# Graph attention on one core: edge attributes in another layout, masks for four tiles at once, one-hots on ScalarE, and second operands of VectorE in PSUM

## The chip, the cores and the metric

The kernel runs on one core of one Trainium2 chip. The metric is the time that the device takes for one execution, in microseconds (us). TensorE (PE) multiplies matrices and loads its weights (PEld); VectorE (DVE) and ScalarE (ACT) work element by element; GpSimd (POOL) here does little but issue gathers, that is, DMAs whose source rows are given by an index; SyncE (SP) issues the other DMAs. SBUF and PSUM are the two on-chip memories.

## The reference

A graph has N = 12500 nodes with 128 features and E = 200000 edges, sorted by their target node. Two layers follow each other, each added to its input:

```python
h = jnp.maximum(_layernorm(x, axis=-1), 0.0)
x = x + _L0_gnn_ref(h, edge_index, edge_attr_32, Wq, Wk, Wv, We)     # attention over edges
h = jnp.maximum(_layernorm(x, axis=-1), 0.0)
x = x + _L1_gnn_ref(h, edge_index, ...)                              # three graph convolutions
```

The change concerns the attention alone:

```python
q = (x @ Wq.T).reshape(N, H, C)          # H = 8 heads, C = 16; k and v alike
edge_bias = edge_attr @ We.T             # (E, 32) @ (32, 8)
scores = jnp.einsum('ehc,ehc->eh', q[dst], k[src]) / np.sqrt(C) + edge_bias
seg_max = jax.ops.segment_max(scores, dst, num_segments=N)
ex = jnp.exp(scores - seg_max[dst])
denom = jax.ops.segment_sum(ex, dst, num_segments=N)
out = segment_sum(v[src] * (ex / denom[dst])[:, :, None], dst)
```

## The kernel before

The program has a general path and a path for graphs whose edges are sorted and evenly spread (`fast()`); the second one runs here. Three stages follow each other.

**Start.** The first edge of each node tile is found (`sv`, `begin`, L193 to L203), and q, k and v of all nodes are computed and written to DRAM (`q_d`, `kv_d`).

**Attention** (L893 to L1132). The nodes are cut into 106 tiles of 118 (`TN`). Each tile takes a window of 2048 edges (`WE`) from the first edge of its nodes on, laid out as 128 partitions times 16 edges (`JJ`). A loop over groups of four tiles prepares masks (`cut`, `con`, `thru`, L976 to L996) and, inside it, each tile does the following. The names are those that the profile's rows show.

- SP loads the edge attributes `ebx` (L1003), the numbers of the target nodes in the tile spread over all partitions, `dw_b` (L1005), and the tile's queries `qt` (L1007). The place of the first edge goes through a one-element copy on ACT (`first_edge`, L929) into a register of SP.
- POOL issues 16 gathers of 128 rows of `kv_d`, 1 KB each (L148, called from `gather`); `kv` has three buffers.
- DVE makes the one-hot `oht` (nodes x edges, L1013). Sixteen matmuls spread the queries to the edges (`qe`, L1019), DVE multiplies them with the keys (L1020) and sums over C (L1023).
- TensorE transposes `ebx` (L1029), ACT copies the result (`et`, L1032), and four matmuls with `wbd` give the bias (L1036), which DVE adds to the scores (L1038).
- ACT spreads the mask `cut` over the heads (`cm`, L1043, L1045). DVE finds the segment maximum by scans along the 16 edges of a partition (L1051, L1053). The ends of the partitions go through TensorE (`ends`, L1058 to L1061), are scanned across the partitions (L1067, L1069) with `th`, a copy that ACT makes of the transposed `thru` (L1065), come back (`far`, L1071, L1072), and the first scans are repeated.
- ACT takes the exponential and writes it into column C of `vals` in SBUF (L1081). DVE multiplies the values with it (L1082, both inputs in SBUF).
- DVE makes the other one-hot, `oh` (edges x nodes, `one_hot`, L677), and sixteen matmuls sum up (`acc`, L1089), which ACT copies to `att` (L1090).

**Sorting beside it.** From the 25th tile on a generator `place_edges` (L680 to L888) does work for the third stage: it sorts 2048 keys of each tile, all 106 tiles side by side in 106 partitions, by two bitonic sorts of 66 exchanges each (`swap`, L700 to L702: one minimum and one maximum over 1024 elements, all operands in SBUF), and then places the result by shifts. `go_on(1)` stands at four places of a tile and advances the generator by one `yield`, which is one exchange, or one of the later instructions.

**Convolutions** (L1190 on): three times, gathers of `t_d` (POOL), one-hots on DVE (`oh`, L1249, whose constant operand `nums` lies in PSUM) and matmuls.

A scheduler sets the order of the instructions of each engine at build time; at run time every engine takes its own in that order and waits by semaphores.

Of the kernel before, what the change touches and what calls it, by code (L numbers as in the profile page):

```python
# [17 lines left out]
P = 128  # L18
D = 128
H = 8  # L20
# [28 lines left out]
def tile_gnn(ctx: ExitStack, tc: tile.TileContext, x, src, dst, ea, wqkvT, weT, w1, w2, w3, par, out):  # L49
# [16 lines left out]
    assert E % RR == 0 and E >= WE and NTT < P and (NTT - 1) * TN + P <= NP  # L66
# [38 lines left out]
    begin = const.tile([1, P], I32, name="begin")  # L105
    way = const.tile([1, 1], I32, name="way")
# [44 lines left out]
    with ExitStack() as s:  # L151
# [44 lines left out]
        nc.vector.tensor_tensor(sv[:, 2 * P:2 * P + NTT], sv[:, 1:NTT + 1], sv[:, 0:NTT], op=ALU.subtract)  # L196
# [5 lines left out]
        nc.vector.tensor_scalar(sv[:, :P], sv[:, :P], float(E - WE), None, op0=ALU.min)  # L202
        nc.vector.tensor_copy(begin, sv[:, :P])  # L203
# [454 lines left out]
    def fast():  # L658
# [21 lines left out]
        def place_edges(rt, ps):  # L680
# [10 lines left out]
            def turned(a, n, o, copy):  # L691

                av = a[:, :n * P].rearrange("t (p c) -> t c p", c=n)
                for c, m in groups(n, 4):
                    tp = ps.tile([P, 4, P], FP, name="et_p")
                    for i in range(m):
                        nc.tensor.transpose(tp[:, i, :NTT], av[:, c + i, :], ident[:NTT, :NTT])
                    copy(o[:, :, c:c + m].rearrange("p t c -> p c t"), tp[:, :m, :NTT])

            def swap(lo, hi, lo2, hi2):  # L700
                nc.vector.tensor_tensor(lo2, lo, hi, op=ALU.min)
                nc.vector.tensor_tensor(hi2, lo, hi, op=ALU.max)  # L702

            def sort(turn):
                size = 2
                while size <= WE:
                    a, b = (x.rearrange("t (n z) -> t n z", z=size) for x in (A[turn], A[1 - turn]))
                    h = size // 2
                    swap(a[:, :, :h], a[:, :, h:][:, :, ::-1], b[:, :, :h], b[:, :, h:][:, :, ::-1])
                    yield  # L710
                    turn = 1 - turn
                    d = h // 2
                    while d:
                        a, b = (x.rearrange("t (n w d) -> t n w d", w=2, d=d) for x in (A[turn], A[1 - turn]))
                        swap(a[:, :, 0], a[:, :, 1], b[:, :, 0], b[:, :, 1])
                        yield
# [43 lines left out]
            mb = ps.tile([P, 2, MG], FP, name="nb")  # L760
            nc.tensor.matmul(mb[0:1, 0, 0:1], sm[:, 3:4], ones[:NTT, 0:1], start=True, stop=True)
            yield
            nc.vector.tensor_scalar(slotted, mb[0:1, 0, 0:1], 0.0, None, op0=ALU.is_equal)
# [121 lines left out]
        with ExitStack() as s:  # L885
# [10 lines left out]
            ps1 = s.enter_context(tc.tile_pool(name="ps1", bufs=1, space=PSUM))  # L896

# [14 lines left out]
            nc.vector.tensor_scalar(shift[:, 1], iota_f, pid[:, 2:3], None, op0=ALU.is_equal)  # L912
            NV = 2
# [12 lines left out]
            def first_edge(bg, t):  # L926


                nc.scalar.copy(bg, begin[:, t:t + 1])  # L929
                return nc.values_load(bg, engines=[mybir.EngineType.SP], min_val=0, max_val=E - WE)  # L930
# [34 lines left out]
            for t0 in range(0, NTT, NG):  # L965
                n = min(NG, NTT - t0)
                if t0 % MG == 0:
# [5 lines left out]
                    if loaded >= NTT and not steps:  # L973
                        steps = place_edges(rt, ps1)
# [10 lines left out]
                    nb = ps1.tile([P, 2, MG], FP, name="nb")  # L985
# [9 lines left out]
                    for m in (con, thru):  # L995
                        nc.vector.tensor_scalar(m[:, :, :mn], m[:, :, :mn], BIG, -BIG, op0=ALU.mult, op1=ALU.add)  # L996
                att = ep.tile([TN, NG, H * (C + 1) + 1], FP, name="att")
                for t in range(t0, t0 + n):
                    i, m = t - t0, t - m0
                    ebx = ld.tile([P, JJ * ED + 1], FP, name="ebx")  # L1000
                    eb = ebx[:, :JJ * ED].rearrange("p (j w) -> p j w", j=JJ)
                    v = first_edge(ebx.bitcast(I32)[0:1, JJ * ED:], t)
                    nc.sync.dma_start(eb, ea[bass.ds(v, WE), :].rearrange("(p j) w -> p j w", j=JJ))  # L1003
# [9 lines left out]
                    nc.vector.tensor_scalar(oht, dw_b, iota_q, None, op0=ALU.is_equal)  # L1013
# [11 lines left out]
                    go_on(1)  # L1025

                    et_p = ps1.tile([P, 4, P], FP, name="et_p")
                    for k in range(4):
                        nc.tensor.transpose(et_p[:, k, :], eb[:, 4 * k:4 * k + 4, :].rearrange("p j w -> p (j w)"),  # L1029
                                            ident)  # L1030
                    et = wk.tile([P, 4, P], FP, name="et")
                    nc.scalar.copy(et, et_p)  # L1032
                    sm = ps1.tile([P, JJ + 2, H], FP, name="sm")
                    bias, far = sm[:, :JJ], sm[:, JJ:]
                    for k in range(4):
                        nc.tensor.matmul(bias[:, 4 * k:4 * k + 4, :].rearrange("p j h -> p (j h)"), et[:, k, :], wbd,  # L1036
                                         start=True, stop=True)
# [3 lines left out]
                    cm = wk.tile([P, H * (JJ + 1) + 1], FP, name="cm")  # L1041
                    W = H * (JJ + 1)
                    nc.scalar.copy(cm[:, :W].rearrange("p (h j) -> p h j", h=H),  # L1043
                                   cut[:, m, :].unsqueeze(1).to_broadcast([P, H, JJ + 1]))
                    nc.scalar.copy(cm[:, W:], cut[:, m, JJ:])  # L1045
# [11 lines left out]
                    ends = ps1.tile([H, 4, P], FP, name="ends")  # L1057
                    nc.tensor.matmul(ends[:, 0, :], mg[:, :, JJ - 1], ident, start=True, stop=True)  # L1058
                    nc.tensor.matmul(ends[:, 1, :], mx[:, :, 0], ident, start=True, stop=True)
                    for k in range(2):  # L1060
                        nc.tensor.matmul(ends[:, 2 + k, :], thru[:, k, m:m + 1].to_broadcast([P, H]), ident,  # L1061
# [388 lines left out]
```

## Time and profile before

| | us |
|---|---|
| time, median of 3 runs (7284.83 to 7306.85) | 7293.77 |
| the profiled execution's own time | 6154.56 |
| its span, first to last instruction | 6152.8 |
| first gather of `kv` begins | 148.2 |
| first and last exchange of the sorts begin | 743.9, 1728.1 |
| last gather of `kv` begins | 2930.9 |
| last copy of `att` (end of the last tile) begins | 2958.1 |

The profiled execution was 1139.2 us shorter than the median of the timed ones; the records do not say why. All durations below are the profiled execution's.

Busy time by stretch, from the profile's windows (first column: stretch in us; then its length, and the busy time of PE, DVE, ACT and POOL; the TensorE clock as a share of full speed; the mean share of the DMA engines that was busy):

| stretch | tiles begun in it | length | PE | DVE | ACT | POOL | clock | DMA |
|---|---|---|---|---|---|---|---|---|
| 148 to 721 | 24 | 573 | 399.95 | 357.29 | 84.00 | 446.40 | 0.72 | 0.58 |
| 721 to 2544 (sorting) | 66 | 1823 | 1165.11 | 1385.66 | 225.80 | 1499.36 | 0.69 | 0.44 |
| 2544 to 2931 | 16 | 387 | 276.01 | 225.00 | 50.85 | 305.37 | 0.69 | 0.48 |
| 2958 to 6153 (convolutions) | | 3195 | 2454.93 | 1297.12 | 598.64 | 1827.63 | 0.88 | 0.82 |

A row of the groups names the source line, the engine, the operation, the tile written and those read, the shapes and the count; after the bar come the busy time in us and the mean duration of one in ns; after the second bar the idle time of the engine just before these instructions, and what ended most of it. "issue" means that the profile shows nothing that the engine waited for. In a timeline each row has its start in us, its duration in us, and then the same names.

### The profile page before, as it was taken

How to read it: one execution, taken by the hardware profiler on the slowest of the kernel's cores; microseconds unless marked ns; L12 is line 12 of the kernel's file. 1: busy time of each engine (PE TensorE's matmuls, PEld its weight loads, DVE VectorE, ACT ScalarE, POOL GpSimd, SP SyncE). 2: the span in 40 equal slices, each digit the busy share in tenths (PEclk: the TensorE clock that was granted, in tenths of full speed). 3: DMA queues.
4: the chain of work that ended last, by engine and by line, in shares of the span. 5: the costliest groups of instructions: out<-in, count | busy, mean ns of one | idle time of the engine just before them, and what ended most of it. 6: DMA issues, size and time to landing. Idle time of an engine off the chain costs nothing. (4 is left out here: it accounts for less than half of the span.)

```text
span 6152.8 us, 80384 instructions
## 1 busy us (share of the span) xinstructions
PE 4406.0 (72%) x28564; PEld 4115.5 (67%) x28564; DVE 3396.2 (55%) x5972; ACT 1011.7 (16%) x2374; POOL 4084.2 (66%) x3617
## 2 busy tenths in 40 slices
PE   6676666666666665767487787877787787778777
PEld 2666655555566665666377777777777776777777
DVE  7566688887876677655243343353343344434344
ACT  3111111110111111111112122111121211112120
POOL 0777788888888888777266566636666664666663
PEclk9677766666676776767788888898888888888888
DMA  6555544433444444454588888878888887888888
GB/s 188 152 143 138 137 112 106 113 103 109 105 128 120 122 112 112 131 132 114 150 214 216 218 216 218 213 209 217 219 216 221 213 211 204 219 219 219 221 215 209
DMA packets 607714, 1051.07 MB, mean 171 GB/s; under 512 B 191227, under 2 KB 418491, under 8 KB 607201
## 3 DMA queue, kind: packets, MB, share of 16 engines
q1 hardware_dynamic: 464311, 695.85, 41.5%
q0 software_dynamic: 142608, 348.39, 23.9%
q8 instruction: 232, 3.80, 0.3%
q14 instruction: 175, 1.43, 0.1%
q10 hardware_dynamic: 388, 1.60, 0.1%
HBM read 773.19 MB, written 272.26 MB: 170 GB/s over the span
## 5 line engine op out<-in xcount | busy, mean ns | idle before, releaser
L148 POOL DMA_INDIRECT rows<-t_d,srcO x1908 | 1827.6, 958 | 1329.2 <-issue 560.2
L148 POOL DMA_INDIRECT kv<-kv_d,srcA x1696 | 2252.3, 1328 | 536.7 <-issue 484.3
L1249 DVE TENSOR_TENSOR oh<-nums,dlS 128x1888 f32<-128x1888 f32 x318 | 674.3, 2121 | 1527.2 <-PE zp L1255 1517.9
L1253 PE MATMUL zp<-oh,mr 128*128 128x118 f32 x6360 | 966.6, 319 | 567.5 <-DMA mr<-m 440.4
L1253 PEld LDWEIGHTS zp<-oh,mr 128*128 128x128 f32 x6360 | 925.5, 233 | 586.4 <-DMA mr<-m 348.7
L1019 PE MATMUL qe<-qt,oht 128*128 128x128 f32 x3392 | 841.4, 415 | 247.3 <-DVE kv L1020 110.7
L1224 PE MATMUL gp<-hs,go 128*117 128x128 f32 x7056 | 891.8, 281 | 125.8 <-DVE go L1221 69.8
L1019 PEld LDWEIGHTS qe<-qt,oht 128*128 128x128 f32 x3392 | 767.1, 310 | 289.7 <-issue 166.8
L1224 PEld LDWEIGHTS gp<-hs,go 128*117 128x117 f32 x7056 | 831.9, 184 | 165.1 <-issue 117.1
L1226 ACT COPY stage<-gp 117x512 f32<-117x512 f32 x1008 | 521.8, 532 | 1375.0 <-PE gp L1224 936.8
L1020 DVE TENSOR_TENSOR kv<-qe,kv 128x512 f32<-128x512 f32 x424 | 289.4, 685 | 678.8 <-DMA kv<-kv_d,srcA 536.8
L1089 PE MATMUL acc<-vals,oh 128*118 128x137 f32 x3392 | 539.8, 329 | 150.5 <-DVE vals L1082 150.0
L1089 PEld LDWEIGHTS acc<-vals,oh 128*118 128x118 f32 x3392 | 522.1, 225 | 171.6 <-DVE vals L1082 171.3
L1221 DVE TENSOR_SCALAR go<-gi,iota_q 128x468 f32<-128x468 uint8 x1008 | 427.8, 456 | 224.5 <-DMA gi<-gi_d 111.8
L1255 PE MATMUL zp<-oh,rows 128*128 128x118 f32 x3816 | 513.2, 288 | 0.2 <-DMA rows<-t_d,srcO 0.2
L1255 PEld LDWEIGHTS zp<-oh,rows 128*128 128x128 f32 x3816 | 492.2, 206 | 0.4 <-DMA rows<-t_d,srcO 0.4
L1058 PE MATMUL ends<-ident,mg 128*8 128x128 f32 x212 | 53.0, 343 | 344.4 <-DVE mg L1053 305.6
L1082 DVE TENSOR_TENSOR vals<-kv,vals 128x2048 f32<-128x2048 f32 x106 | 242.3, 2286 | 27.2 <-ACT vals L1081 26.8
L1058 PEld LDWEIGHTS ends<-ident,mg 128*8 128x8 f32 x212 | 11.7, 96 | 366.1 <-DVE mg L1053 298.8
L1023 DVE TENSOR_REDUCE sc<-kv 128x128 f32<-128x2048 f32 x106 | 240.8, 2272 | 0.0
L677 DVE TENSOR_TENSOR oh<-iota_f,dlA 128x1888 f32<-128x1888 f32 x106 | 224.0, 2113 | 5.0 <-PE acc L1089 5.0
L1036 PE MATMUL sm<-wbd,et 128*128 128x32 f32 x848 | 167.8, 351 | 45.0 <-DVE mg L1075 37.7
(242 smaller groups left out, 3648.1 us busy)
## 6 DMA issues: line engine op xcount, KB each, us to landing
m<-stage SPq DMA_DIRECT2D x252, 784.0 KB
mr<-m SPq DMA_DIRECT2D x318, 560.0 KB
dw_b<-dlb_d SPq DMA_DIRECT2D x106, 512.0 KB
gi<-gi_d SPq DMA_DIRECT2D x252, 204.8 KB
rows<-t_d,srcO POOLq DMA_INDIRECT x1908
kv<-kv_d,srcA POOLq DMA_INDIRECT x1696
ebx<-in_edge_attr_dram SPq DMA_DIRECT2D x106, 256.0 KB
mr<-m SPq DMA_DIRECT2D x318, 75.0 KB
```

The source lines that it names most:

```text
L148: nc.gpsimd.indirect_dma_start(out=o, out_offset=None, in_=table[:, :], in_offset=bass.IndirectOffsetOnAxis(ap=idx, axis=0))
L1019: nc.tensor.matmul(qe[:, k, :], ohv[:, :, j + k], qt, start=True, stop=True)
L1020: nc.vector.tensor_tensor(qk[:, j:j + 4, :], qe, qk[:, j:j + 4, :], op=ALU.mult)
L1023: nc.vector.tensor_reduce(sc.rearrange("p h j -> p j h"), qk.rearrange("p j (h c) -> p j h c", h=H), AX.X, ALU.add)
L1082: nc.vector.tensor_tensor(vh[:, :, :, :C], kv[:, :, D:].rearrange("p j (h c) -> p j h c", h=H), vh[:, :, :, C:].to_broadcast([P, JJ, H, C] ...
L1089: nc.tensor.matmul(acc, oh[:, j, :], va[:, j, :], start=(j == 0), stop=(j == JJ - 1))
L1221: nc.vector.tensor_scalar(go[:, :n], gv[:, a:a + n], iota_q, None, op0=ALU.is_equal)
L1224: nc.tensor.matmul(gp[:, i, :], go[:, i].rearrange("p t k -> p (t k)"), hs[:, g * SG + a + i, :], start=True, stop=True)
L1226: nc.scalar.copy(stage[:, a:a + n, :], gp[:, :n, :])
L1249: nc.vector.tensor_tensor(oh, nums.unsqueeze(1).to_broadcast(sh), dlS[:, t, :].unsqueeze(2).to_broadcast(sh), op=ALU.is_equal)
L1253: nc.tensor.matmul(zp[:, i, :], mr[:q, j, :], oh[:q, j, :], start=False, stop=False)
L1255: nc.tensor.matmul(zp[:, i, :], rows[:, j, :], oh[:, RC + j, :], start=False, stop=(j == JO - 1))
```

## The change

- **Edge attributes.** A second input holds the attributes transposed: row 32·i + w, column e holds attribute w of edge 4·e + i. A tile loads 128 rows of 512 columns (`eaT`), 256 KB as before, and multiplies them with `wbd` directly; the four transposes and the copy `et` go. The first edge of a tile is rounded down to a multiple of 4 for this (`begin4`).
- **Masks.** `cm` and `th` are made for a group of four tiles ahead (`cms`, two `th2`), not once a tile.
- **One-hots on ACT.** `oht` and `oh` are made by ACT as relu(1 - |x - y|): an Abs with a bias per partition and a Relu in place; `oh` needs 16 of the Abs, one for each edge of a partition.
- **Exponentials in PSUM.** ACT writes the exponentials to PSUM (`ex`), DVE multiplies the values from there, and ACT copies `ex` into `vals`.
- **Sort halves in PSUM.** Each exchange is cut into two halves. For each, ACT copies the upper operand to PSUM (`hc`, one buffer), a `yield` follows, and DVE takes minimum and maximum of an SBUF and a PSUM operand. `go_on` advances six steps a tile in place of four.
- **PSUM.** `ends` and the tile `sm` (bias, `far`, `ex`) have two buffers each, `acc` one.

```diff
             def swap(lo, hi, lo2, hi2):
-                nc.vector.tensor_tensor(lo2, lo, hi, op=ALU.min)
-                nc.vector.tensor_tensor(hi2, lo, hi, op=ALU.max)
+                n, d = lo.shape[1:]
+                for k in range(2):
+                    cut = (slice(None), slice(k * n // 2, (k + 1) * n // 2)) if n > 1 else (
+                        slice(None), slice(None), slice(k * d // 2, (k + 1) * d // 2))
+                    hc = ps.tile([P, WE // 4], FP, name="hc")[:NTT].rearrange(
+                        "t (n d) -> t n d", n=max(1, n // 2))
+                    nc.scalar.copy(hc, hi[cut])
+                    yield
+                    nc.vector.tensor_tensor(lo2[cut], lo[cut], hc, op=ALU.min)
+                    nc.vector.tensor_tensor(hi2[cut], lo[cut], hc, op=ALU.max)
...
+            def where_zero(x):
+                nc.scalar.activation(x, x, AF.Relu, bias=ones[:, 0:1], scale=-1.0)
...
+                    cms = mk.tile([P, MG, W + 1], FP, name="cms")
+                    nc.scalar.copy(cms[:, :mn, :W].rearrange("p m (h j) -> p m h j", h=H),
+                                   cut[:, :mn].unsqueeze(2).to_broadcast([P, mn, H, JJ + 1]))
+                    nc.scalar.copy(cms[:, :mn, W:], cut[:, :mn, JJ:])
+                    ths = {}
+                    for a, b in groups(mn, 2):
+                        th2 = mk.tile([H, 2, 2, P], FP, name="th2")
+                        ends = ps2.tile([P, 4, P], FP, name="ends")[:H]
+                        for i in range(2 * b):
+                            nc.tensor.matmul(ends[:, i, :], thru[:, i % 2, a + i // 2:a + i // 2 + 1]
+                                             .to_broadcast([P, H]), ident, start=True, stop=True)
+                        nc.scalar.copy(th2[:, :b].rearrange("h m k p -> h (m k) p"), ends[:, :2 * b])
...
-                    nc.sync.dma_start(eb, ea[bass.ds(v, WE), :].rearrange("(p j) w -> p j w", j=JJ))
+                    nc.sync.dma_start(eb, eaT[:, bass.ds(v, WE // 4)])
...
-                    nc.vector.tensor_scalar(oht, dw_b, iota_q, None, op0=ALU.is_equal)
+                    nc.scalar.activation(oht, dw_b, AF.Abs, bias=niota[:, 0:1])
+                    where_zero(oht)
...
-                    go_on(1)
-                    et_p = ps1.tile([P, 4, P], FP, name="et_p")
+                    go_on(2)
+                    sm = ps2.tile(shared, FP, name="sm")
+                    bias, far, ex = sm[:, :JJ], sm[:, JJ:JJ + 2], sm[:, JJ + 2:]
                     for k in range(4):
-                        nc.tensor.transpose(et_p[:, k, :], eb[:, 4 * k:4 * k + 4, :].rearrange("p j w -> p (j w)"),
-                                            ident)
-                    et = wk.tile([P, 4, P], FP, name="et")
-                    nc.scalar.copy(et, et_p)
...
-                        nc.tensor.matmul(bias[:, 4 * k:4 * k + 4, :].rearrange("p j h -> p (j h)"), et[:, k, :], wbd,
-                                         start=True, stop=True)
+                        nc.tensor.matmul(bias[:, 4 * k:4 * k + 4, :].rearrange("p j h -> p (j h)"),
+                                         eb.rearrange("a (p k) -> a k p", k=4)[:, k, :], wbd, start=True, stop=True)
...
-                    nc.scalar.activation(vh[:, :, :, C], mx.rearrange("p h j -> p j h"), AF.Exp)
+                    nc.scalar.activation(ex, mx.rearrange("p h j -> p j h"), AF.Exp)
                     nc.vector.tensor_tensor(vh[:, :, :, :C], kv[:, :, D:].rearrange("p j (h c) -> p j h c", h=H),
-                                            vh[:, :, :, C:].to_broadcast([P, JJ, H, C]), op=ALU.mult)
+                                            ex.unsqueeze(3).to_broadcast([P, JJ, H, C]), op=ALU.mult)
+                    nc.scalar.copy(vh[:, :, :, C], ex)
                     go_on(1)
                     oh = wk.tile([P, JJ, TN], FP, name="oh")
-                    one_hot(oh, dlA[:, t, :])
-                    acc = ps2.tile([TN, H * (C + 1) + 1], FP, name="acc")
+                    for j in range(JJ):
+                        nc.scalar.activation(oh[:, j, :], iota_f[:, :TN], AF.Abs, bias=dlA[:, t, j:j + 1], scale=-1.0)
+                    where_zero(oh)
+                    acc = ps1.tile([TN, H * (C + 1) + 1], FP, name="acc")
```

## The prediction

> **What bounds the kernel now.** The chain of waits of the page tells nothing here: it ends after five short steps. I read first the costliest groups, then the timeline, then the windows.
>
> ```profile
> L148 POOL DMA_INDIRECT rows<-t_d,srcO x1908 | 1827.6, 958 | 1329.2 <-issue 560.2
> L148 POOL DMA_INDIRECT kv<-kv_d,srcA x1696 | 2252.3, 1328 | 536.7 <-issue 484.3
> ```
>
> Second row: POOL's gathers of the attention. Busy 2252.3 plus idle 536.7 is 2789 us, and by their first and last start they last from 148.2 to 2930.9, 2783 us. So POOL does nothing but issue gathers, one after another with 0.305 us between, and nearly never waits: **attention is as long as 1696 gathers take to issue.** Nothing of the third stage starts before it ends, so a microsecond saved there is one saved in all. The first row is the same instruction in the convolutions: 958 ns in place of 1328. Why, the timeline shows, first in attention, then in a convolution:
>
> ```profile
> 342.31 0.95 POOL L148 DMA_INDIRECT kv<-kv_d,srcA  x1 [0.30 <-issue]
> 343.56 0.95 POOL L148 DMA_INDIRECT kv<-kv_d,srcA  x1 [0.30 <-issue]
> 343.89 2.29 DVE L1082 TENSOR_TENSOR vals<-kv,vals 128x2048 f32<-128x2048 f32 x1 [3.11 <-ACT vals L1081]
> ...
> 344.82 2.19 POOL L148 DMA_INDIRECT kv<-kv_d,srcA  x1 [0.30 <-issue]
> ...
> 347.31 0.94 POOL L148 DMA_INDIRECT kv<-kv_d,srcA  x1 [0.30 <-issue]
> ```
>
> The convolution:
>
> ```profile
> 4004.05 2.12 DVE L1249 TENSOR_TENSOR oh<-nums,dlS 128x1888 f32<-128x1888 f32 x1 [1.97 <-PE zp L1255]
> ...
> 4004.50 0.94 POOL L148 DMA_INDIRECT rows<-t_d,srcO  x1 [0.30 <-issue]
> 4005.74 0.94 POOL L148 DMA_INDIRECT rows<-t_d,srcO  x1 [0.30 <-issue]
> ```
>
> The gather at 344.82, issued while DVE multiplies two SBUF operands, ends 0.83 us after DVE does; its neighbours take 0.95. In the convolution, under a DVE operation as long but with one operand in PSUM (`nums`), gathers keep 0.94. I set all 1696 gathers of the timeline against DVE's intervals: the 648 that meet L1082, L677, L1013, L701 or L702 take 1849 ns in the mean, the 1048 others 1006. Above the usual 947 that is 584 us for the first and 62 us for the second. These five lines are what the change takes out of VectorE's SBUF operands.
>
> By the windows a tile takes 573/24 = 23.9 us at first, 1823/66 = 27.6 beside the sorting, 387/16 = 24.2 at the end.
>
> **POOL after the change.** L1082 and the exchanges get a PSUM operand, L677 and L1013 leave DVE. Nearest row for the first two: L1020, kv<-qe,kv, has one PSUM and one SBUF input; fitted over all gathers, a gather loses about a tenth of its overlap with it, against nine tenths for L1082. So all gathers should come to the mean of the unhindered 1048: 16 x (1.006 + 0.305) = 21.0 us a tile. The ends: 16 x (0.947 + 0.305) = 20.0 if nothing hinders, 27.6 in the sorting if PSUM operands hindered as well. I take 21.0; scans (L1051, L1053), L1078 and the placing after the sorts keep two SBUF inputs and are in it. All 1696: 2223 us against 2783, **560 us less, if no other engine is slower than 21 us a tile.**
>
> Here the Trainium skill speaks against the change. "SBUF — State Buffer", Who interferes with whom, says that VectorE with two SBUF inputs holds up only GpSimd instructions that read SBUF, and infers that descriptor generation, being a write, is held up by two-port modes alone. By that rule only L1013 (tensor_scalar on bf16, 106 x 1.28 = 136 us at most) would matter, and the change would bring about 100 us. The rows above contradict it: L1082 is a tensor_tensor, and the gather under it took 2.19 us. I go by the trace.
>
> **ACT.** Rows to price from, of ACT's groups within the attention:
>
> ```profile
> L1032 ACT COPY et<-et_p 128x512 f32<-128x512 f32 x106 | 62.1, 586 | 551.2 <-PE sm L1036 472.2 <-PE et_p L1029 78.9
> L1081 ACT ACTIVATE vals<-mg 128x128 f32<-128x128 f32 x104 | 44.5, 428 | 27.2 <-DVE mg L1078 25.9
> L1126 ACT ACTIVATE hg<-xg,rs 118x128 f32<-118x128 f32 x100 | 41.2, 482 | 132.0 <-DVE rs L1122 132.0
> L1065 ACT COPY th<-ends 8x256 f32<-8x256 f32 x105 | 38.0, 362 | 394.8 <-PE ends L1061 394.8
> ```
>
> From L1065 to L1032, 256 elements more cost 224 ns, 0.875 ns each. So 2048 elements are 586 + 1536 x 0.875 = 1.93 us, 1888 are 1.79. `oht`: two passes, 3.86. `oh`: sixteen Abs over 118 elements; L1126 (118 x 128, two pointers) starts every 0.386 us in a row, so at most 6.2 us; "ScalarE: Activation LUTs", What ACT_TABLE_LOAD costs, takes 93 ns off for one pointer less, an estimate of 4.7; I take 5.0, and the Relu 1.79. The copy of `ex` is priced like L1081, 0.43; `Exp` stays. Gone are `et` 0.59, `th` 0.36, `cm` 0.49, against two copies like L1032 and one `cms` per four tiles, about 0.5. ACT now has 360.66/106 = 3.4 us a tile; after: 3.4 - 1.44 + 3.86 + 5.0 + 1.79 + 0.43 + 0.5 = 13.5. In the sorting six `hc` copies of 512 elements come on top; nearest row 0.586 (end above: 1.2, at the 1.9 ns that an element of the strided L1081 costs beyond its start): 3.5, so **17.0 us**. That is below 21, but no longer idle.
>
> The same page's rules for authors say to use VectorE, not ScalarE, for relu and the like. Rows: DVE makes both one-hots in 1.28 + 2.11 = 3.4 us, ACT needs 10.65. By the rule the edit loses 7 us of engine time a tile, 770 us in all; but ACT was busy 13% of the attention and DVE's 3.4 us sit on POOL, which sets the pace. By the trace the edit gains, as long as ACT stays below POOL.
>
> **DVE.** Now 14.9 us a tile (357.29/24) outside the sorting, 21.0 in it. The one-hots go: 11.5. In the sorting six half exchanges a tile, each two operations like L1020 at 0.685: 8.2, so **19.7 us** (somewhat less, since successive operations overlap by some 0.08). All 132 exchanges cost 4 x 0.685 - 2.42 = 0.32 more each, 43 us over the whole, beside POOL. Six steps a tile with twice the yields per exchange: the sorts take 264/6 = 44 tiles (before, 984 us), the placing fewer than before, and the generator ends near the same tile; nothing spills over the end.
>
> **PE.** The transposes go (L1029: 424, 105.8 us); the same matmuls on `thru` are only moved to the group. PE's 1841.07 us become some 1735, 16.4 a tile. The weights `eb` are read with a step of four elements; `oht` is read with sixteen, and its loads (310 ns against 225 for `acc`) hide beside matmuls. DMAs: as many, as large; their share of 0.44 to 0.58 rises by the shorter tile to 0.6 to 0.67, and the convolutions reach 0.82 on the same engines. SP's queue keeps its order; its register loads wait for the one-element ACT copies, now behind operations of up to 1.93 us, with two tiles of lead. Five small DVE instructions for `begin4` cost about 1 us ahead of the first gather. One `acc` buffer: the next tile's sum waits for the ACT copy of the last, a tile earlier.
>
> **The new wait.** An `hc` copy needs DVE to have finished with the one buffer; in ACT's queue one-hots and `Exp` stand behind it, and TensorE waits for those. DVE's minimum needs the copy; queued behind it are scans, score products and the `vals` product that frees `kv`. Six round trips a tile: two half operations 1.37, copy 0.59. Other work between two trips: DVE (19.7 - 8.2)/6 = 1.9 us, ACT (17.0 - 3.5)/6 = 2.3. If they mesh perfectly, a trip costs about 3.3 to 3.5 us and a tile 20 to 21; if half of the copies stand behind an ACT operation of 1.9 us with little else to do on DVE, about 3 us a tile are added. I take **23.3 in the sorts, 22 in the placing, 21 elsewhere**: 44 x 23.3 + 22 x 22 + 40 x 21 = 2349 us against 2783, 434 less. In the profiled execution 6154.56 becomes about 5720.
>
> The runs' median is 1139.2 us above the profiled execution, and no view says why. Carried over unscaled, 434 us give 6860; scaled by 7293.77/6154.56 = 1.185, 514 us give 6780. I take the middle, **6820**.
>
> **Rivals.**
> - *POOL alone sets the pace* (18%): DVE and ACT mesh; 560 to 660 less, 6630 to 6730. For it: in the sorting before DVE was busy 76% and POOL did not wait. Against it: two more engines at 80 to 94%.
> - *The handing over of `hc` sets the pace, yet below the old one* (18%): 25 to 27 us a tile while sorting; 66 x (27.6 - 26) + 40 x 2.9 = 222 less, 7070.
> - *Slower* (13%): the same hand-over, each copy behind a long ACT operation. With 19.7 us of DVE work and six idle times a tile, the sorting tile passes the point where the other tiles' 116 us are eaten at 27.6 + 116/66 = 29.4 us, that is at 1.6 us idle per copy. With 2.5 us (a 1.93 us Relu and the copy) it is 34.7: 66 x 7.1 - 116 = 353 more, 7650. Against it: DVE's scans and products usually stand between.
> - *It does not do what it says*: the skill's rule holds, -100 us at best, or PSUM operands hinder too (3%, counted as no change).
>
> **Chances.** Main case 48%. A change within 0.3% (22 us) is about what a measurement of this kernel can't tell from none. Faster 84%, same 3%, slower 13%. The range 6600 to 7190 leaves out the slower case and the weakest of the partial ones; the main case's own range is 6720 to 6920.
>
> **What would show it.** Gathers of `kv` near 1.0 us in place of 1.33; POOL's idle time before them up, ended by DVE (a `kv` buffer not free) in the sorting if hand-over slips; ACT busy about 2200 us in place of 1011.7; the last gather starting near 2500. Wrong would be: gathers that stay at 1.3 us, ACT rows above 2.5 us for 2048 elements, or DVE idle more than 1.6 us before each minimum.

## The result, and the profile after

The changed kernel takes 7762.7 us (median of 4 runs, 7753.7 to 7795.7) where the kernel before takes 7289.3 (7274.2 to 7306.9) on the same chip: a ratio of **1.068 [1.064, 1.071]**. It is slower; the forecast was 6820 us.

What the change says it does, it did. Of the profile page after, the costliest groups that answer to those shown before (line, engine, operation, tiles, shapes, count; busy us, mean ns; idle us before, and what ended most of it):

```profile
L149 POOL DMA_INDIRECT rows<-t_d,srcO x1908 | 1823.7, 956 | 2328.9 <-PE zp L1184 666.8
L149 POOL DMA_INDIRECT kv<-kv_d,srcA x1696 | 1695.3, 1000 | 1696.5 <-DVE vals L1104 847.0
...
L1114 PE MATMUL acc<-vals,oh 128*118 128x137 f32 x3392 | 616.9, 352 | 507.7 <-ACT vals L1106 263.4
...
L1056 DVE TENSOR_TENSOR kv<-qe,kv 128x512 f32<-128x512 f32 x424 | 285.4, 678 | 565.5 <-remote 357.9
...
L1115 ACT COPY att<-acc 118x137 f32<-118x137 f32 x106 | 29.0, 273 | 921.4 <-remote 452.3
```

Second row: a gather of `kv` takes 1000 ns in place of 1328, so POOL issues all 1696 in 557 us less. But its idle time went from 536.7 to 1696.5 us, and half of that is now ended by the `vals` product, which frees a `kv` buffer: POOL no longer sets the pace. No other engine does so by its work alone: of the 3431 us of attention TensorE is busy 1907, VectorE 1662 and ScalarE 1512. The word "remote" at the last two rows is new: the first profile of the kernel before has no such wait. It is what the profile writes where the awaited signal came, but so late (over 1.5 us after the recorded end of every instruction that sends it) that it names no sender. The first row, the convolutions' gathers, is untouched by the change, yet waits 2328.9 us where the profile before had 1329.2.

ACT's groups have the sizes that the prediction gave them:

```profile
L1110 ACT ACTIVATE oh<-iota_f,dlA 128x118 f32<-128x118 f32 x1696 | 510.3, 382 | 0.0
L1048 ACT ACTIVATE oht<-dw_b,niota 128x2048 f32<-128x2048 bf16 x106 | 211.7, 1998 | 95.7 <-PE qe L1055 58.9 <-remote 33.1 <-issue 2.9
...
L930 ACT ACTIVATE oh<-oh,ones 128x1888 f32<-128x1888 f32 x106 | 197.2, 1860 | 7.2 <-remote 6.1 <-ACT oh L1110 0.6 <-ACT oht L1048 0.4
L712 ACT COPY hc<-A 106x512 f32<-106x512 f32 x264 | 156.6, 593 | 334.7 <-DVE A L715 268.7 <-issue 37.2 <-DVE A L714 21.6
```

Where the time goes is seen in the timeline of the changed kernel (start, duration, engine, line; in brackets the idle time before and what ended it), here ahead of the sorting:

```profile
400.24 2.28 DVE L1104 TENSOR_TENSOR vals<-kv,sm 128x2048 f32<-128x2048 f32 x1
...
400.88 0.95 POOL L149 DMA_INDIRECT kv<-kv_d,srcA  x1 [0.30 <-issue]
...
402.55 0.38 ACT L1106 COPY vals<-sm 128x128 f32<-128x128 f32 x1 [5.30 <-issue]
...
404.13 1.03 PE L1055 MATMUL qe<-qt,oht 128*128 128x128 f32 x4
404.64 0.94 POOL L149 DMA_INDIRECT kv<-kv_d,srcA  x1 [0.30 <-issue]
405.42 0.01 SPq L958 DMA_DIRECT2D srcA<-in_src_dram  x1
405.89 0.95 POOL L149 DMA_INDIRECT kv<-kv_d,srcA  x1 [0.30 <-issue]
406.85 0.70 SPq L959 DMA_DIRECT2D dwx<-dstf_d  x1
...
433.42 0.95 POOL L149 DMA_INDIRECT kv<-kv_d,srcA  x1 [0.30 <-issue]
434.28 0.28 ACT L1115 COPY att<-acc 118x137 f32<-118x137 f32 x1 [31.05 <-remote]
...
434.61 5.54 PE L1114 MATMUL acc<-vals,oh 128*118 128x137 f32 x29 [29.44 <-issue]
...
444.21 0.69 DVE L1056 TENSOR_TENSOR kv<-qe,kv 128x512 f32<-128x512 f32 x1 [33.08 <-PE qe L1055]
```

and in the windows over the gap (busy us and number of instructions of each engine, granted clock, DMA share):

```profile
core 0: us, PE busy (x) PEld busy (x) DVE busy (x) ACT busy (x) POOL busy (x), PEclk, DMA share, GB/s
...
404.00:434.00 30.00, 1.16 (x7) 0.97 (x5) 0.61 (x3) 0.00 (x0) 22.68 (x25) 0.56 0.43 111
```

The last matmul of a sum ends at 404.30, the next tile's sum needs the one `acc` buffer, and ACT's copy out of it comes 30 us later. TensorE's 12 records of that window (weight loads included) all lie before 405.2; after them it records nothing for 29.4 us, VectorE three instructions and ScalarE none, and SP issues one load in 1.4 to 8.4 us, in place of one in about 0.5. Only POOL works on, one gather per 1.25 us. VectorE stands idle for over 10 us in one piece 52 times in the 106 tiles (three times in the first profile before). Attention, from the first gather to the last copy of `att`, takes 3431 us in this execution.

**Two kinds of chip.** Five further series of runs, each on another chip, always had the kernel before beside them. On four chips it took 7286 to 7389 us, on one 6150 (medians; on one chip single runs lie within 1.2% of each other). Each chip had one series, so what is called a kind of chip here could also be a condition of the machine at that hour; no run tells the two apart. The profile that the prediction was read from shows 6154.56, like the odd one; the times it was to forecast are of the other kind. So before anything else the kernel before was profiled again.

### The profile page after: what moved, and what is told of

It is laid out like the page before. It is cut to its first block, busy times and chain, and to the rows that moved or that the text cites. A ratio compares the mean times of both kernels' runs of the same rounds, so it can differ in the third digit from the quotient of the medians.

```text
span 7766.9 us, 81306 instructions
## 1 busy us (share of the span) xinstructions
PE 4783.1 (62%) x28140; PEld 4417.7 (57%) x28140; DVE 3091.8 (40%) x6028; ACT 2165.5 (28%) x4439; POOL 3523.3 (45%) x3617
## 5 line engine op out<-in xcount | busy, mean ns | idle before, releaser
L149 POOL DMA_INDIRECT rows<-t_d,srcO x1908 | 1823.7, 956 | 2328.9 <-PE zp L1184 666.8
L149 POOL DMA_INDIRECT kv<-kv_d,srcA x1696 | 1695.3, 1000 | 1696.5 <-DVE vals L1104 847.0
L1249 PE MATMUL gp<-hs,go 128*117 128x128 f32 x7056 | 1078.6, 312 | 689.0 <-issue 506.3
L1278 PE MATMUL zp<-oh,mr 128*128 128x118 f32 x6360 | 1057.7, 337 | 602.6 <-DMA mr<-m 317.6
L1249 PEld LDWEIGHTS gp<-hs,go 128*117 128x117 f32 x7056 | 979.9, 212 | 772.4 <-issue 617.1
L1278 PEld LDWEIGHTS zp<-oh,mr 128*128 128x128 f32 x6360 | 1014.6, 251 | 623.3 <-issue 356.8
L1110 ACT ACTIVATE oh<-iota_f,dlA 128x118 f32<-128x118 f32 x1696 | 510.3, 382 | 0.0
L1066 PE MATMUL sm<-wbd,ebx 128*128 128x32 f32 x848 | 209.9, 393 | 160.2 <-DMA sw_d<-srcA 62.6
L1066 PEld LDWEIGHTS sm<-wbd,ebx 128*128 128x128 f32 x848 | 208.7, 328 | 162.5 <-issue 125.1
L712 ACT COPY hc<-A 106x512 f32<-106x512 f32 x264 | 156.6, 593 | 334.7 <-DVE A L715 268.7
L1104 DVE TENSOR_TENSOR vals<-kv,sm 128x2048 f32<-128x2048 f32 x106 | 241.5, 2278 | 9.0 <-ACT sm L1103 4.4
```

Source lines behind the costliest of these rows:

```text
L149: nc.gpsimd.indirect_dma_start(out=o, out_offset=None, in_=table[:, :], in_offset=bass.IndirectOffsetOnAxis(ap=idx, axis=0))
L1110: nc.scalar.activation(oh[:, j, :], iota_f[:, :TN], AF.Abs, bias=dlA[:, t, j:j + 1], scale=-1.0)
L1249: nc.tensor.matmul(gp[:, i, :], go[:, i].rearrange("p t k -> p (t k)"), hs[:, g * SG + a + i, :], start=True, stop=True)
L1278: nc.tensor.matmul(zp[:, i, :], mr[:q, j, :], oh[:q, j, :], start=False, stop=False)
```

## Experiments

### First series (kernel before: 7365.6 us)

`again_before` is the kernel before. `onehots_dve` takes both one-hots back to VectorE, `sort_sbuf` the exchanges back to SBUF (with `go_on(1)`), `both_back` does both:

```diff
-                    nc.scalar.activation(oht, dw_b, AF.Abs, bias=niota[:, 0:1])
-                    where_zero(oht)
+                    nc.vector.tensor_scalar(oht, dw_b, iota_q, None, op0=ALU.is_equal)
...
-                    for j in range(JJ):
-                        nc.scalar.activation(oh[:, j, :], iota_f[:, :TN], AF.Abs, bias=dlA[:, t, j:j + 1], scale=-1.0)
-                    where_zero(oh)
+                    one_hot(oh, dlA[:, t, :])
...
-                    yield from swap(a[:, :, :h], a[:, :, h:][:, :, ::-1], b[:, :, :h], b[:, :, h:][:, :, ::-1])
+                    swap(a[:, :, :h], a[:, :, h:][:, :, ::-1], b[:, :, :h], b[:, :, h:][:, :, ::-1])
+                    yield
```

> The kernel before, unchanged, for a profile that belongs to the timed runs. Theory S (the first profile of before, 6153 us, was an execution without TensorE's late progress that the profile of the changed kernel shows): span near 7290 us, convolutions near 4180 us in place of 3195, attention (first gather to last att copy) 2950 to 3150 us. Rival (the convolutions of the changed kernel are slower because of the change): the convolutions stay near 3200 us and the span cannot be explained by them.

> The changed kernel with both one-hots back on VectorE (tensor_scalar and tensor_tensor as before), all else as changed. Theory A (ScalarE's order of work, with 10.6 us of one-hots a tile in front of Exp, vals and att copies, delays TensorE and so the release of kv): attention falls from 3430 us to 2750 or less and the time to 7050 to 7200, below the kernel before. Theory B (the hand-over of hc): no more than 100 us change, 7650 to 7760. Theory S alone (late TensorE, whatever the order): about 7700.

> The changed kernel with the exchanges of the sorts as before (two SBUF operands, one yield each, four steps a tile). Theory B: the tiles beside the sorting fall from 31 us to 25, the time to about 7350. Theory A: the tiles without sorting take 33.6 us in the changed kernel too, so the sorting is not the cause; within 100 us of 7763, and gathers in the sorting become longer.

> The changed kernel with one-hots on VectorE and exchanges as before; what stays of the change is the layout of the attributes, the masks for four tiles and the exponentials in PSUM. Theory A: near the kernel before, 7100 to 7300, since only the product of the values no longer holds up gathers (about 190 us less of hindrance) and no ScalarE queue is added. If it stays above 7500, the cause lies in the remaining parts: the tile sm that is shared by bias, far and ex, or one buffer of acc.

Measured: `again_before` 7374.7 us (1.002 [1.000, 1.004]), `onehots_dve` 7582.4 (1.028 [1.020, 1.036]), `sort_sbuf` 7814.6 (1.059 [1.053, 1.066]), `both_back` 7534.7 (1.022 [1.017, 1.028]).

The kernel before spends 2963 us in attention and 4232 in the convolutions on this chip, against 2810 and 3194 in its first profile, while the mean gather differs little (1298 against 1328 ns, and 955 against 958 in the convolutions). So 1038 us of the 1139 that the prediction could not place lie in the convolutions. They are not only waits: TensorE's granted clock there is 0.79 in place of 0.88, and its busy time 2766 us in place of 2455. And the changed kernel (4182 there) doesn't lengthen them: its loss is all in attention, 3431 against 2963.

The hand-over of `hc`, the prediction's slower rival, is not the cause: without it attention stays at 3420 us, and the 24 tiles ahead of the sorting are as slow as those beside it (33.9 and 32.0 us a tile in the changed kernel). The one-hots are a half: 3184 us of attention without them, still more than before, while the range expected was missed. This run alone does not say that ScalarE's time is the reason, for with VectorE's one-hots back the gathers take 1125 ns in place of 1000, so that their pace changes too. What `both_back` keeps (layout, masks, `ex` in PSUM, one `acc`) costs 2.2% on its own.

### Second series (kernel before: 6150.5 us)

`acc_two` is `both_back` with two `acc` buffers, `ex_back` is `both_back` with the exponentials written into `vals` and not copied, `layout_masks` is both, `before_acc1` is the kernel before with one `acc` buffer:

```diff
-                    acc = ps1.tile([TN, H * (C + 1) + 1], FP, name="acc")
+                    acc = ps2.tile([TN, H * (C + 1) + 1], FP, name="acc")
...
-                    nc.scalar.activation(ex, mx.rearrange("p h j -> p j h"), AF.Exp)
+                    nc.scalar.activation(vh[:, :, :, C], mx.rearrange("p h j -> p j h"), AF.Exp)
...
-                                            ex.unsqueeze(3).to_broadcast([P, JJ, H, C]), op=ALU.mult)
-                    nc.scalar.copy(vh[:, :, :, C], ex)
+                                            vh[:, :, :, C:].to_broadcast([P, JJ, H, C]), op=ALU.mult)
```

> The kernel of both_back (one-hots on VectorE, exchanges as before; it took 1.022 of the time before) with two acc buffers again, in the PSUM bank that hc leaves free. Theory L (the pace is the latency of a tile: a kv buffer is held for its 16 gathers and for the time from the last gather to the vals product, 52 us there, and there are three of them; the single acc buffer lengthens that time, since the sum of the next tile, and all that stands behind it on TensorE, waits for ScalarE's copy to att): a ratio of 0.99 to 1.005, the last gather to vals near 42 us. Theory M (the copy of the exponentials into vals, behind other work on ScalarE, is what lengthens it): no change, 1.02. Theory N (layout and masks): no change, 1.02.

> The kernel of both_back with the exponentials written straight into vals in SBUF, as before, and no copy of them; one acc buffer stays. Theory M (the copy of ex stands between the vals product and the sum, and waits on ScalarE): a ratio of 0.99 to 1.01, although the gathers that meet the vals product are held up again (some 30 us in all of POOL's time more). Theory L (acc): 1.02 to 1.03, for the gathers get slower and nothing gets faster.

> Both of these together: what is left of the change is the layout of the attributes, the masks for four tiles ahead, and two buffers each for ends and sm. Theories L and M: 1.00 or a little below (0.98 to 1.00), since four transposes and the copies et, cm and th are gone from a tile. Theory N (layout or masks cost: ebx is held until the bias products and not only until the transposes, so that the loads behind it on SP's queue start later): 1.015 to 1.025 still.

> The kernel before with one acc buffer in place of two, nothing else. Theory L: slower, 1.01 to 1.02 (80 to 150 us). Theories M and N: the time before within 0.3%, since POOL sets the pace there and the sum of a tile is far behind the vals product that frees the kv buffer.

Measured: `acc_two` 5992.9 us (0.974 [0.972, 0.976]), `ex_back` 6149.8 (1.000 [0.999, 1.001]), `layout_masks` 6146.5 (0.999 [0.998, 1.000]), `before_acc1` 6150.9 (1.000 [0.999, 1.001]). This chip turned out to be the other kind, so none of these ratios may be set against those of the first series. By itself the series says two things. The second `acc` buffer alone is worth nothing to the kernel before. And where the exponentials are in PSUM the gathers take 1233 ns in place of 1330; 1696 x 0.097 = 165 us, and attention is shorter by 159 (2648 against 2807). **For this part of the change the prediction's sum holds on this chip: what POOL saves is saved.** In these traces not one wait of VectorE or ScalarE in attention ends by "remote".

### Third series (kernel before: 7388.6 us)

`after_again`, `onehots_again` and `acc_two_again` repeat the kernels of these names; `hc_acc2` is `onehots_dve` with two `acc` buffers and one for `ends`. 

```diff
-                    ends = ps2.tile([P, 4, P], FP, name="ends")[:H]
+                    ends = ps1.tile([P, 4, P], FP, name="ends")[:H]
...
-                    acc = ps1.tile([TN, H * (C + 1) + 1], FP, name="acc")
+                    acc = ps2.tile([TN, H * (C + 1) + 1], FP, name="acc")
```

> The changed kernel once more. In one series the kernel before took 7366 us, in the next 6150; the two series may have run on different chips, and in the traces of the second TensorE and ScalarE show hardly any of the late waits (a signal seen long after the recorded end of what it waits for) of the first. Theory C (the change loses by these late waits, since its tile leans on round trips between TensorE, ScalarE and VectorE): if the kernel before takes about 6150 here, the changed one takes 5650 to 6000 (ratio 0.92 to 0.975); if it takes about 7350, the ratio is 1.06 to 1.07 again. Theory W (ScalarE's added work is too slow for the chain in any case): a ratio above 1.02 in both.

> The changed kernel with both one-hots back on VectorE, once more (1.028 where the kernel before took 7366 us). Theory C: with the kernel before at 6150, about 0.95 to 0.97 (the gathers meet the two one-hots again, some 130 us of POOL's time more than in the changed kernel's); at 7350, 1.02 to 1.03. Theory W: clearly faster than the changed kernel in both.

> acc_two once more (0.974 where the kernel before took 6150). With the kernel before at 6150: 0.97 to 0.98 again. At 7350, theory L (one acc buffer lets TensorE wait for ScalarE's late copy): 0.98 to 1.005; else 1.02 as both_back.

> The changed kernel with both one-hots on VectorE and two acc buffers, for which ends has one buffer; exchanges and exponentials stay in PSUM. Theory C: with the kernel before at 6150, 0.94 to 0.96, as the gathers meet only the two one-hots and attention is 16 x (1.10 + 0.305) x 106 = 2380 to 2500 us; at 7350, 1.00 to 1.02, below onehots_again by the second acc buffer.

Measured: `after_again` 7866.3 us (1.065 [1.061, 1.070]), `onehots_again` 7573.0 (1.028 [1.023, 1.034]), `acc_two_again` 7516.6 (1.018 [1.013, 1.023]), `hc_acc2` 7585.1 (1.029 [1.023, 1.035]). The kernel that won 2.6% on the chip of the second series loses 1.8% here, on the same instructions. Two `acc` buffers don't help: 1.018 against 1.022 of `both_back` (another chip), and 1.029 against 1.028 of `onehots_again` (where `ends` has lost a buffer for it), both inside the intervals. Theory L falls with that. Whether the changed kernel loses on the other kind of chip too stays open: none of its runs came to one.

By now the runs lay in an odd order: the shorter the gathers, the longer the attention. Two causes were put against each other, a chain of hand-overs that has become too long (H), and the pace of the gathers itself (G).

### Fourth series (kernel before: 7383.6 us)

`after_paced` is the changed kernel with more work for POOL, a memset that the gather then overwrites. `ex_two` is `acc_two` with a second Exp in place of the copy, so that nothing stands behind the `vals` product:

```diff
+                        nc.gpsimd.memset(kv[:, j, :D], 0.0)
                         gather(kv[:, j, :], kv_d, srcA[:, t, j:j + 1])
```

```diff
                     nc.scalar.activation(ex, mx.rearrange("p h j -> p j h"), AF.Exp)
+                    nc.scalar.activation(vh[:, :, :, C], mx.rearrange("p h j -> p j h"), AF.Exp)
...
-                    nc.scalar.copy(vh[:, :, :, C], ex)
```

> The changed kernel beside the other three. With the kernel before at 7290 to 7390: 1.06 to 1.07 by every theory. With it at 6150: theory C (late signals are what the change loses by) 0.92 to 0.975, theory W (ScalarE's added work is too slow in any case) above 1.02.

> The changed kernel with a POOL memset of 128 x 128 elements of the kv buffer ahead of each gather, which overwrites it: POOL spends about 0.3 us more per gather, 16 x (1.0 + 0.305 + 0.3) = 25.7 us a tile, the pace that it had before the change. With the kernel before at 7290 to 7390: theory G (gathers issued faster make the other engines' signals later): faster than the changed kernel, 1.00 to 1.04. Theory H (the chain of hand-overs is too long, whatever POOL does): as slow as the changed kernel or slower, 1.065 to 1.09, since a kv buffer is held 5 us longer. With the kernel before at 6150: about 0.97 to 1.00 by both.

> acc_two (1.018 where the kernel before took 7389 us, 0.974 where it took 6150) with the copy of ex replaced by a second Exp straight into vals: the sum waits for nothing behind the vals product, and the gathers stay as fast as in acc_two. At 7290 to 7390: theory H (the copy's hop): 0.99 to 1.005; theory G: 1.015 to 1.02. At 6150: 0.97 to 0.98 by both.

> layout_masks once more (0.999 where the kernel before took 6150): the attributes' layout, the masks for four tiles ahead and two buffers for ends and sm, everything else as before. At 7290 to 7390: theories G and H: 0.99 to 1.005. If it is above 1.01, the layout or the masks cost, and the ex parts are not the rest of the loss.

Measured: `after_third` 7856.7 us (1.064 [1.058, 1.069]), `after_paced` 7706.7 (1.043 [1.038, 1.048]), `ex_two` 7560.0 (1.022 [1.016, 1.028]), `layout_again` 7328.8 (0.993 [0.991, 0.995]).

`ex_two` is no faster than `acc_two_again` (1.018), so the copy of `ex` isn't what costs. Between `layout_again` and `ex_two` lie the place of the exponentials that the product reads and one more Exp a tile, and with that place the gathers' mean, 1304 and 1195 ns: 3% of the time. VectorE's score products, from the groups of `layout_again` and then of `ex_two`, show what changes:

```profile
L1049 DVE TENSOR_TENSOR kv<-qe,kv 128x512 f32<-128x512 f32 x424 | 288.6, 684 | 573.3 <-DMA kv<-kv_d,srcA 335.3 <-PE qe L1048 99.6 <-remote 69.5
```

```profile
L1049 DVE TENSOR_TENSOR kv<-qe,kv 128x512 f32<-128x512 f32 x424 | 286.8, 681 | 483.1 <-remote 237.0 <-PE qe L1048 78.9 <-DMA kv<-kv_d,srcA 64.1
```

In the first VectorE waits for gathered data, as it must where POOL sets the pace. In the second it hardly does, and waits for late signals in their place.

`after_paced` became faster by 150 us by adding work to POOL. H expected it slower, so H falls as the whole cause.

### Fifth series (kernel before: 7285.6 us)

The memset is made twice as large, and nothing else in the program is changed:

```diff
-                        nc.gpsimd.memset(kv[:, j, :D], 0.0)
+                        nc.gpsimd.memset(kv[:, j, :], 0.0)
```

> The changed kernel beside after_paced2. With the kernel before at 7290 to 7390: 1.06 to 1.07. With it at 6150: theory C (it loses by late signals, which are rare there) 0.92 to 0.975, theory W (ScalarE's added work is too slow in any case) above 1.02.

> after_paced with a memset of twice the size (128 x 256), an estimated 0.42 us from the 0.224 us of 128 x 128[...]: POOL needs 16 x (1.0 + 0.305 + 0.42 + 0.05) = 28.4 us a tile, a little above its pace before the change, so 106 x 28.4 = 3010 us of attention is the least there can be (before: 2963). Theory G: 1.015 to 1.035, below the 1.043 of after_paced. Theory H: above 1.05. With the kernel before at 6150: 1.03 to 1.04, for POOL alone sets the pace.

Measured: `after_fourth` 7758.7 us (1.067 [1.061, 1.072]), **`after_paced2` 7052.3 (0.968 [0.964, 0.973])**: 706 us faster than the changed kernel, and faster than the kernel before, below every range that was given. It holds the changed kernel whole, and 0.33 us more work for POOL per gather (0.42 had been estimated). POOL's groups, and VectorE's score products, first of `after_paced`:

```profile
L149 POOL DMA_INDIRECT kv<-kv_d,srcA x1696 | 1699.4, 1002 | 434.8 <-issue 393.2 <-POOL kv L1045 39.7 <-DMA kv<-kv_d,srcA 1.4
L1045 POOL MEMSET kv<- 128x128 f32 x1696 | 314.2, 224 | 864.2 <-DVE vals L1105 825.5 <-DMA dw_b<-dlb_d 29.9 <-DMA srcA<-in_src_dram 7.2
```

```profile
L1057 DVE TENSOR_TENSOR kv<-qe,kv 128x512 f32<-128x512 f32 x424 | 287.1, 681 | 574.3 <-issue 218.5 <-remote 172.6 <-DMA kv<-kv_d,srcA 61.4
```

and then of `after_paced2`:

```profile
L149 POOL DMA_INDIRECT kv<-kv_d,srcA x1696 | 1712.5, 1010 | 426.2 <-issue 309.1 <-POOL kv L1045 107.8 <-DMA kv<-kv_d,srcA 8.6
L1045 POOL MEMSET kv<- 128x256 f32 x1696 | 496.1, 331 | 55.4 <-DVE vals L1105 55.1
```

```profile
L1057 DVE TENSOR_TENSOR kv<-qe,kv 128x512 f32<-128x512 f32 x424 | 289.4, 684 | 665.1 <-DMA kv<-kv_d,srcA 495.9 <-PE qe L1056 88.7 <-PE acc L1115 20.0
```

With 0.11 us more per gather POOL's wait for a free buffer goes from 864 to 55 us, and VectorE waits for gathers again. POOL sets the pace as before the change, at (2860 - 150)/106 = 25.6 us a tile. ScalarE, VectorE and TensorE keep up with it, one-hots, `hc` copies, the copy of `ex` and the single `acc` buffer included.

A memset on POOL also lets the scheduler order the other engines' instructions anew, which is a rival to the pace. The traces settle it for the start of attention. By operation, tiles and shapes, TensorE, VectorE, ScalarE and SP have the same order in `after`, `after_paced` and `after_paced2` up to the ninth `vals` product, and only POOL's differs. These are the three ninth products:

```profile
541.78 2.28 DVE L1104 TENSOR_TENSOR vals<-kv,sm 128x2048 f32<-128x2048 f32 x1
529.09 2.28 DVE L1105 TENSOR_TENSOR vals<-kv,sm 128x2048 f32<-128x2048 f32 x1
442.63 2.28 DVE L1105 TENSOR_TENSOR vals<-kv,sm 128x2048 f32<-128x2048 f32 x1
```

From the first gather (at 153.25, 151.90 and 150.2) they end after 390.8, 379.5 and 294.7 us (the changed kernel beside the paced ones, on their chips: `after_third` 397.9, `after_fourth` 388.4; the kernel before, in its own order: `again_before` 307.5). Between the two paced kernels the order is the same up to the fifteenth, which ends after 558.9 and 427.5 us. So the step between the two memsets is there without any change of order. Farther on the orders differ at many places, and nothing separates the two causes.

Profiled executions, one for each kernel (`ex_back` and `before_acc1` left out), sorted by the time between two gathers (counted from the traces: mean of a gather; mean time from start to start where gathers follow within 3 us; first gather to last `att` copy; POOL's waits over 0.6 us there, ahead of gathers and of their memsets; sum of VectorE's and ScalarE's waits that end by "remote"):

| kernel | ratio | gather ns | start to start us | attention us | POOL waits us | late us |
|---|---|---|---|---|---|---|
| after | 1.068 | 1000 | 1.294 | 3431 | 1204 | 1549 |
| sort_sbuf | 1.059 | 1070 | 1.331 | 3420 | 1064 | 1791 |
| hc_acc2 | 1.029 | 1109 | 1.384 | 3193 | 783 | 947 |
| onehots_dve | 1.028 | 1125 | 1.388 | 3184 | 746 | 1023 |
| ex_two | 1.022 | 1195 | 1.408 | 3178 | 618 | 1080 |
| after_paced | 1.043 | 1002 | 1.412 | 3344 | 890 | 1249 |
| acc_two_again | 1.018 | 1206 | 1.418 | 3151 | 570 | 1056 |
| both_back | 1.022 | 1214 | 1.423 | 3134 | 541 | 725 |
| again_before | 1.002 | 1298 | 1.461 | 2963 | 232 | 494 |
| layout_again | 0.993 | 1304 | 1.478 | 2964 | 220 | 477 |
| after_paced2 | 0.968 | 1010 | 1.514 | 2710 | 88 | 78 |
| second series: acc_two | 0.974 | 1233 | 1.443 | 2648 | 18 | 0 |
| second series: layout_masks | 0.999 | 1330 | 1.488 | 2807 | 14 | 0 |

(The memsets come two by two, so the gathers of `after_paced` start 1.26 and 1.47 us apart in turn, those of `after_paced2` 1.26 and 1.68; the table has means.) On the slow kind of chip attention falls as the gathers move apart, but for `after_paced`, which is nearly as slow as the kernels that share its one-hots on ACT. In that kernel late waits fall from 1249 us at 1.41 to 78 at 1.51; kernels that were not paced still have 477 at 1.48.

**What is shown:** on this kind of chip the changed kernel loses by the pace of its gathers. More work on POOL takes the whole loss away, in the first tiles with the order of the other engines unchanged, and the parts that were suspected (`hc`, the copy of `ex`, the single `acc`, ScalarE's one-hots) are still there when it is gone. **What is not shown:** why signals come late. A possible course is that once POOL has had to wait, its gathers follow without a pause, the others fall behind, and POOL has to wait again; that could make the steep step between the two memsets. It is argued, not tested: runs of over 20 gathers without a pause cover only 27% of the changed kernel's attention. How much of the gain over the whole attention comes from the new order is not known either.

## Why the prediction was wrong, step by step

- **Gathers held up by VectorE's SBUF operands: right.** 1.006 us was forecast, 1.000 measured; at the gather of 400.88, issued while L1104 multiplies with its operand in PSUM, the duration is 0.95. The rule of the Trainium skill ("SBUF — State Buffer", Who interferes with whom), by which only about 100 us were to be had, is contradicted by POOL's own busy time, 557 us less.
- **ScalarE's prices: right.** Busy 2165.5 us (some 2200 forecast). The passes over 2048 elements took 2.00 and 1.99 us (1.93), the Relu of `oh` 1.86 (1.79), the sixteen Abs 510.3/106 = 4.8 us (5.0), `hc` 0.593 (0.586). The rule for authors in "ScalarE: Activation LUTs" of the Trainium skill, VectorE for relu and the like, has a point here that the prediction passed over: on one chip the ratio is 1.065 with the one-hots on ScalarE (`after_again`) and 1.028 without (`onehots_again`). But `after_paced2` is faster than the kernel before with the same one-hots on ScalarE.
- **`hc`'s hand-over at 23.3 us a tile: not the cause,** as `sort_sbuf` shows, though ScalarE stands idle for 334.7 us before these copies, most of it ended by VectorE. In `after_paced2` tiles beside the sorting take 24.8 us with all hand-overs in them.
- **One `acc` buffer, the copy of `ex`, strided weights, SP's queue at nothing:** the first two were tried and cost nothing that could be measured; the strided weights go with `layout_again`, which is 0.7% faster than the kernel before, and SP's queue behind ScalarE's one-hots with `after_paced2`.
- **The step that failed: "560 us less, if no other engine is slower than 21 us a tile."** It was settled by adding up busy times: ScalarE 17.0, VectorE 19.7, TensorE 16.4, all below 21. The sums were about right (over the whole attention 14.3, 15.7 and 18.0 us a tile were measured; the 17.0 and 19.7 are for tiles beside the sorting, outside it 13.5 and 11.5 were forecast), but the condition is not one of busy time. With gathers every 1.29 us a tile takes 32 us though no other engine works more than 18 in it, and the same work keeps up with 25.6 when gathers come every 1.51 us. The pace of POOL was taken as something that only others can limit; here it limits them.
- **The second failure: carrying the difference over.** The 1139 us between profile and median were halved between "unscaled" and "scaled", as if they were a property of the chip apart from the change. The runs point to late waits behind both: 1038 us of the difference lie in the convolutions, where VectorE's and ScalarE's waits that end by "remote" sum to 1053 us in `again_before` and to none in the first profile, and whose gathers had been unhindered (958 ns) all along. The change gave attention such gathers too. That both have one cause was not tested, and the lower granted clock of TensorE in these convolutions (0.79 against 0.88) is not explained. With the one profile there was, this could not be read; but a profile 16% faster than the times is of another behaviour, and the forecast's 13% for "slower" was given to `hc` alone.
- The range (6600 to 7190) missed by 573 us, and the slower rival's 7650 is near by luck: its mechanism is another, and its sum counts copies of `hc` in 66 tiles where the same text has them in 44.

## What to carry to other kernels

If a profile's own time lies far from the timed runs, settle that first (profile again, on another chip) and forecast nothing from it before; a change can win on one chip and lose on the next. Making the engine that sets the pace faster is only worth what the others can take, and that can be tested by slowing it: the kernel that got faster when its pace-setter was given idle work told more here than undoing parts one by one. Such an edit can change the order of the other engines too, so compare the orders in the traces. Busy sums below the pace are a necessary condition, not a sufficient one, where tiles pass through several in-order queues with few buffers.

## What was not expected of the hardware

Chips differ: the same program took 6150 us on one and 7286 to 7389 on four others, with nearly equal gathers (`kv` 1331 ns in `before_acc1` and 1298 in `again_before`, the convolutions' 958 and 955) and no "remote" waits at all on the first. On the others two matmuls of one sum, with nothing to wait for between them, start more than 0.5 us apart 15 times in the attention of the kernel before, 103 times in the changed one's, 138 times in `after_paced`, twice in `after_paced2`, and never in the traces of the first chip.

On one of these chips a memset of 0.33 us ahead of each gather was worth 706 us. The convolutions issue their gathers at the unhindered pace on all chips and take 3188 to 3201 us on the one and 4163 to 4268 on the others, in `after_paced2` too (4192), whose memsets stand in attention alone. Whether pacing would help there was not tried.
